# Edge-gated graph layer on one core: edges packed in tiles of 128 per 64 targets instead of a loop over list slots

## The chip, the cores and the metric

The kernel runs on one core of a Trainium2 chip. The metric is the device time of one execution in microseconds (us), as the median of several runs. The profile is one further execution with the hardware profiler on. The core's engines, each with its own instruction stream, are TensorE (PE; its weight loads are listed apart as PEld), VectorE (DVE), ScalarE (ACT), GpSimd (POOL) and SyncE (SP), which here only starts DMAs. SBUF is the on-chip memory, PSUM the memory that TensorE writes its products to, DRAM the memory off the core.

## What is computed

The input `x` holds 16 batches of 1024 nodes with 256 features (h below), in float32; `adj` is a 1024 x 1024 matrix that is zero except for some 9,000 edges.

```python
pre_u = einsum('bud,dk->buk', h, W1[:256])
pre_v = einsum('bvd,dk->bvk', h, W1[256:])
hidden = relu(pre_u[:, :, None, :] + pre_v[:, None, :, :] + b1)
S   = sigmoid(einsum('buvk,ko->buvo', hidden, W2)[..., 0] + b2[0])
a_t = einsum('buv,bud->bvd', S * adj, h)
m_t = einsum('uv,bud->bvd', adj, h) * h
z   = beta1*h + beta2*(a_t @ Wa + ba) + beta3*(m_t @ Wm + bm)
```

The gate S of a pair (u, v) matters only where adj is not zero. With the reference's own inputs there are 9,052 such pairs; the longest list of sources of one target has 19, and of the sixteen groups of 64 consecutive targets the fullest holds 607 edges, the emptiest 549.

## The kernel before

There are two stages. The first runs over the 16 batches. For each it makes three matrix products on TensorE: `pt` (L141: h times W1's upper half and Wa side by side, which goes to `tab` and to a DRAM table of 4 batches), `pp` (L147: h times W1's lower half, which goes to `pv`), and `pm` (L161: the dense product of h with the whole `adj`, 1024 x 1024, which gives m), whose result times Wm (`pz`, L171) makes z except for the gated sum. `pv` and z go to DRAM.

The second stage is the edge loop. It takes 128 targets at a time, one per partition, 8 blocks in all. A hardware loop (L245 to L247) does 4 slots of every target's list in a turn, as many turns as the longest of the 128 lists needs; in the profiled execution that is 35 turns. In a turn VectorE finds the next four sources of each target (`top`, L202; `pick`, L217; `key`, L219). Then come four rounds, one per group of 4 batches. In a round GpSimd starts four indirect DMAs (L211), each of which fetches one row of 8 KB per partition, namely the source's W1 part and its Wa part for 4 batches. VectorE adds `pv` (L223) and, batch by batch, takes relu, multiplies with W2 and sums (L225). ScalarE makes the gate (L228) and, for each batch and slot, a diagonal 128 x 128 matrix `dg` (L235). TensorE multiplies each `dg` with the fetched Wa part and sums into `pa` (L237), 16 products of 128 x 256 a round, and VectorE adds `pa` to z (L238). A partition whose list has ended fetches nothing and weighs 0, but all instructions run over it.

The order of the instructions on each engine is fixed when the program is built, by a scheduler that looks at the dependences and at the buffers of each pool; eight `fetched` buffers and two `pa` buffers are what lets rounds overlap, and nothing overlaps from one turn to the next beyond them. All products are float32, and each is executed as two MATMUL instructions with a weight load each.

Of the kernel before, what the change touches and what calls it, by code (L numbers as in the profile page):

```python
# [13 lines left out]
P = 128  # L14
# [3 lines left out]
def kernel(  # L18
# [32 lines left out]
    HB = 512  # L51
    GB = 4
    NG = B // GB
    TS = 4
    NGB = 8
    assert D == 256 and N % HB == 0
# [4 lines left out]
    table = [dram.tile([N, GB * 2 * D], FP, name=f"table{g}") for g in range(NG)]  # L61
    pv_dram = dram.tile([N, B * D], FP, name="pv_dram")
    z_dram = dram.tile([N, B * D], FP, name="z_dram")

    def rows(src, n):
        return bass.AP(tensor=src.tensor, offset=src.offset, ap=[[0, P], [1, n]])

    def load_rows(src, n, name):
        t = const.tile([P, n], FP, name=name)
        nc.scalar.dma_start(t, rows(src, n))  # L70
        return t
# [3 lines left out]
    adjT_sb = const.tile([P, NT, N], FP, name="adjT_sb")  # L75
    w2_b = load_rows(W2, D, "w2_b")
    b2_b = load_rows(b2, 1, "b2_b")
    turns = const.tile([P, NT], I32, name="turns")
    ukey = const.tile([P, N], FP, name="ukey")
    nc.gpsimd.iota(ukey, pattern=[[-1, N]], base=N, channel_multiplier=0,  # L80
                   allow_small_or_imprecise_dtypes=True)

# [1 line left out]
    with ExitStack() as s1:  # L84
        wp = s1.enter_context(tc.tile_pool(name="wp", bufs=1))
# [44 lines left out]
        for b in range(B):  # L130
            h, hT = hs
            if b + 1 < B:
                hs = load_h(b + 1)
# [107 lines left out]
    for vt in range(NT):  # L241
        pv, z, key = block
        if vt + 1 < NT:
            block = load_block(vt + 1)
# [37 lines left out]
```

## Time and profile before

| | us |
|---|---|
| median of 3 runs | 3558.36 (3556.51 to 3566.06) |
| profiled execution, span | 3569.1 |
| TensorE busy | 2179.8 (61%) |
| VectorE busy | 2148.4 (60%) |
| ScalarE busy | 929.8 (26%) |
| GpSimd busy | 659.6 (18%) |

The profiled execution is 10.7 us (0.3%) longer than the median of the runs. The page cuts the span into 40 slices of 89 us and gives each engine's busy share in tenths. [...] "Idle before" is how long an engine stood still just before the instructions of a group, and the releaser is what ended it. The two stages are easy to tell apart in the slices: TensorE is full in the first eleven, and half full after that.

### The profile page before, as it was taken

What the parts mean: (1) busy time and instruction counts of PE and PEld (TensorE: products, weight loads), DVE (VectorE), ACT (ScalarE), POOL (GpSimd) and SP (SyncE); (2) the same over time, 40 slices, a digit from 0 to 9 for tenths busy, and PEclk for the clock granted to TensorE, in tenths of its full rate; (3) what the DMA queues carried; (4) which work ended last, traced back from release to release, by engine and by line L of the source; (5) the groups of instructions that cost most, each with busy time, mean ns of one, the idle gap of its engine ahead of it and who ended that gap; (6) DMA issues with size and microseconds to landing.
All of it is one profiled execution on the core that took longest, in us unless ns stands there. A gap on an engine that the chain in (4) does not pass through costs nothing. (4 is left out here: it accounts for less than half of the span.)

```text
span 3569.1 us, 27584 instructions
## 1 busy us (share of the span) xinstructions
PE 2179.8 (61%) x7040; PEld 1527.9 (43%) x7040; DVE 2148.4 (60%) x6077; ACT 929.8 (26%) x2672; POOL 659.6 (18%) x568
## 2 busy tenths in 40 slices
PE   8999999999355355445445544555544545535554
PEld 4555555555244244434334433444433434434443
DVE  3122122221776777766877776777678767677776
ACT  1010110110133233333233332333323323323332
POOL 0000000000221322212222222222122322222222
PEclk9999999999667767767677776677666867776777
DMA  6233233322642253063245202530641064135300
GB/s 229 106 133 114 106 106 128 120 106 83 268 188 74 90 208 120 24 257 151 70 182 210 74 15 113 225 131 26 258 162 59 5 237 179 63 123 220 135 15 25
DMA packets 174748, 458.50 MB, mean 128 GB/s; under 512 B 46832, under 2 KB 113904, under 8 KB 136432
## 3 DMA queue, kind: packets, MB, share of 16 engines
q0 software_dynamic: 80640, 296.79, 22.4%
q1 hardware_dynamic: 41888, 92.28, 7.0%
q10 hardware_dynamic: 52160, 68.69, 5.5%
q8 instruction: 30, 0.49, 0.1%
q14 instruction: 30, 0.25, 0.0%
HBM read 664.27 MB, written 83.89 MB: 210 GB/s over the span
## 5 line engine op out<-in xcount | busy, mean ns | idle before, releaser
L237 PE MATMUL pa<-fetched,dg 128*128 128x256 f32 x4480 | 1295.8, 460 | 1363.4 <-ACT dg L235 1363.4
L237 PEld LDWEIGHTS pa<-fetched,dg 128*128 128x128 f32 x4480 | 1046.4, 237 | 1612.8 <-ACT dg L235 1419.7
L211 POOL DMA_INDIRECT fetched<-table,idx x560 | 657.6, 1174 | 2821.8 <-DVE idx L204 1807.5
L225 DVE SCALAR_TENSOR_TENSOR hid<-hid,w_b 128x256 f32<-128x256 f32 x2240 | 823.6, 420 | 15.6
L235 ACT ACTIVATE dg<-ident,wt 128x128 f32<-128x128 f32 x2240 | 744.7, 392 | 282.6 <-PE pa L237 187.8
L223 DVE TENSOR_TENSOR hid<-fetched,pv_blk 128x1024 f32<-128x1024 f32 x560 | 683.0, 1220 | 114.0 <-DMA fetched<-table,idx 111.1
L238 DVE TENSOR_TENSOR z_blk<-pa,z_blk 128x1024 f32<-128x1024 f32 x140 | 171.4, 1224 | 511.2 <-PE pa L237 511.2
L161 PE MATMUL pm<-adj_sb,h 128*128 128x512 f32 x1024 | 442.1, 592 | 0.0
L228 ACT ACTIVATE gate<-sc,b_b 128x16 f32<-128x16 f32 x140 | 43.0, 307 | 1253.6 <-DVE hid L225 1253.5
L161 PEld LDWEIGHTS pm<-adj_sb,h 128*128 128x128 f32 x1024 | 194.6, 190 | 238.1 <-issue 237.3
L163 DVE TENSOR_TENSOR mT<-pm,hT 128x512 f32<-128x512 f32 x64 | 44.2, 691 | 386.7 <-PE pm L161 386.7
L141 PE MATMUL pt<-w_tab,hT 128*128 128x512 f32 x512 | 243.8, 599 | 12.0 <-DMA w_tab<-in_Wa_dram 12.0
L143 ACT ACTIVATE tab<-pt 128x256 f32<-128x256 f32 x128 | 49.2, 384 | 754.4 <-PE pt L141 754.4
L149 DVE TENSOR_TENSOR pv<-pp,b_b 128x256 f32<-128x256 f32 x128 | 54.1, 423 | 240.6 <-PE pp L147 240.6
L217 DVE SCALAR_TENSOR_TENSOR pick<-ukey,top,adjT_sb 128x1024 f32<-128x1024 f32 x140 | 180.1, 1287 | 2.5
L225 DVE DVE_READ_ACCUMULATOR hid<-hid,w_b 128x1 f32 x2240 | 180.2, 80 | 0.0
L147 PE MATMUL pp<-w_v,hT 128*128 128x256 f32 x512 | 131.7, 380 | 3.9 <-DVE pv L149 3.9
L141 PEld LDWEIGHTS pt<-w_tab,hT 128*128 128x128 f32 x512 | 98.2, 192 | 80.9 <-issue 74.3
L228 ACT ACT_TABLE_LOAD x35 | 44.9, 1283 | 321.8 <-DVE hid L225 157.3
L147 PEld LDWEIGHTS pp<-w_v,hT 128*128 128x128 f32 x512 | 97.5, 191 | 72.9 <-issue 61.5
L171 PE MATMUL pz<-w_m,mT 128*128 128x256 f32 x512 | 113.1, 379 | 0.0
L171 PEld LDWEIGHTS pz<-w_m,mT 128*128 128x128 f32 x512 | 91.2, 189 | 26.1 <-issue 7.7
(25 smaller groups left out, 327.0 us busy)
## 6 DMA issues: line engine op xcount, KB each, us to landing
table<-tab ACTq DMA_DIRECT2D x16, 2048.0 KB, 7.0
hT<-in_xT_dram SPq DMA_DIRECT2D x16, 1024.0 KB, 7.4
h<-in_x_dram SPq DMA_DIRECT2D x16, 1024.0 KB, 5.5
pv_dram<-pv ACTq DMA_DIRECT2D x16, 1024.0 KB, 9.4
z_dram<-z ACTq DMA_DIRECT2D x16, 1024.0 KB, 4.4
pv_blk<-pv_dram SPq DMA_DIRECT2D x8, 2048.0 KB, 8.4
z_blk<-z_dram SPq DMA_DIRECT2D x8, 2048.0 KB, 15.0
out_dram<-z_blk SPq DMA_DIRECT2D x8, 2048.0 KB, 37.3
```

Source lines behind the costliest of these rows:

```text
L141: nc.tensor.matmul(pt, hT[:, c, nt * P:(nt + 1) * P], w_tab[:, c, :], start=(c == 0), stop=(c == DC - 1))
L147: nc.tensor.matmul(pp, hT[:, c, nt * P:(nt + 1) * P], w_v[:, c, :], start=(c == 0), stop=(c == DC - 1))
L161: nc.tensor.matmul(pm, h[:, ut, c * P:(c + 1) * P], adj_sb[:, ut, v0:v0 + HB], start=(ut == 0), stop=(ut == NT - 1))
L171: nc.tensor.matmul(pz, mT[:, c, nt * P:(nt + 1) * P], w_m[:, c, :], start=(c == 0), stop=(c == DC - 1))
L211: nc.gpsimd.indirect_dma_start(out=tiles[t], out_offset=None, in_=table[g], in_offset=bass.IndirectOffsetOnAxis(ap=idx[:, t:t + 1], axis=0 ...
L217: nc.vector.scalar_tensor_tensor(pick, ukey, top[:, t:t + 1], adjT_sb[:, vt, :], ALU.is_equal, ALU.mult, accum_out=val[:, t:t + 1])
L223: nc.vector.tensor_tensor(hid, f[:, :, 0, :], pv[:, g * GB:(g + 1) * GB, :], ALU.add)
L225: nc.vector.scalar_tensor_tensor(hid[:, b, :], hid[:, b, :], 0.0, w2_b, ALU.max, ALU.mult, accum_out=sc[:, b, t:t + 1])
L228: nc.scalar.activation(gate, sc, AF.Sigmoid, bias=b2_b)
L235: nc.scalar.activation(dg, ident, AF.Copy, scale=wt[:, b, t:t + 1])
L237: nc.tensor.matmul(pa[:, b, :], dg, f[:, b, 1, :], start=(t == 0), stop=(t == TS - 1))
L238: nc.vector.tensor_tensor(z[:, g * GB:(g + 1) * GB, :], pa, z[:, g * GB:(g + 1) * GB, :], ALU.add)
```

## The change

The dense product with `adj` and the loop over slots are gone. The program is straight-line code for the given shape.

**Lists.** `lists(vt)`, once per block of 128 targets, builds from `adj` the packed lists of its two *windows* of 64 targets. VectorE takes the 24 largest keys of every target (three rounds of `max`); short TensorE products count and place them; each window gets 640 *slots* in 5 tiles of 128, one edge per partition. For every slot there result the source's row number (`uidx`), the edge's value (`val`, fetched from DRAM by ten indirect DMAs of 4 bytes per partition per block), a 0/1 matrix `mark` (which slots belong to which of the 64 targets, kept in DRAM as `who`), and `whose` (slot by target, with the value in it). What does not fit (a list over 24, a window over 640) is done by a loop behind a branch at the end of the program, L372, which is skipped if nothing is left over.

**Tables.** `rows(g, nt)` makes, for 4 batches and 128 nodes, h times W1's halves. The upper half goes to the DRAM table, beside which `copy_h` puts h itself; the lower half stays in SBUF as `pv`, with the targets' two halves swapped for two of the 4 batches (`hs`). Table and `pv` of group g+1 are made during the edges of group g, block by block.

**Edges.** `edges(g, vt, pv)` goes over 2 windows of 5 tiles, 320 tiles in all. Per tile there is one indirect DMA of 128 rows of 8 KB (five `fetched` buffers); two products `pc`, which hand each slot its target's `pv` row, each from 64 partitions only, one from the lower 64 and one from the upper; VectorE's add and four relu-multiply-sums as before; one sigmoid; five ScalarE copies that fill `left` (64 columns with the plain value, 64 with value times gate, for each of 4 batches); and four products into `acc`, which sum m and a side by side (m in 64 of the 128 partitions, a in the other 64). Per window `acc` is read out (`ev`: m times h on VectorE, a on ScalarE) and transposed by 8 TensorE instructions into `LT` (4 ScalarE copies). Per block, 16 products with Wm and Wa give z (L341), which is stored at once.

```diff
-    TS = 4
-    NGB = 8
+    W = 64
+    NW = P // W
+    TW = 5
+    E = TW * P
+    S = 24
...
+    def lists(vt):
...
+        nc.vector.tensor_scalar(key, adj_b, 0.0, None, ALU.not_equal, ALU.add, accum_out=count)
+        nc.vector.tensor_tensor(key, key, ukey, ALU.mult)
+        for s in range(0, S, 8):
+            nc.vector.max(top[:, s:s + 8], key)
+            if s + 8 < S:
+                nc.vector.scalar_tensor_tensor(key, key, top[:, s + 7:s + 8], key, ALU.is_lt, ALU.mult)
...
+        for w in range(NW):
...
+            nc.vector.tensor_scalar(early, slot, Rv[:, 0:1], None, ALU.is_lt)
+            mark = big.tile([P, E], FP, name="mark")
+            nc.vector.scalar_tensor_tensor(mark, slot, first, early, ALU.is_ge, ALU.mult)
+            nc.sync.dma_start(who[i], mark)
...
+            for j in range(TW):
+                nc.gpsimd.indirect_dma_start(
+                    out=val[:, i, j:j + 1], out_offset=None, in_=adj_flat,
...
+            for j in range(TW):
+                nc.vector.tensor_scalar(whose[:, i, j, :], place, L[:, j, 4:5], val[:, i, j:j + 1],
+                                        ALU.is_equal, ALU.mult)
...
+    def rows(g, nt):
...
+        for h in range(2):
+            pu = small("pu")
...
+                    nc.tensor.matmul(pu[:, bb * D:(bb + 1) * D], hT[:, 2 * h + bb, c, :], w_u[:, c, :],
...
+            nc.scalar.copy(tab[:, 2 * h * D:(2 * h + 2) * D], pu)
...
+                    left = hs[:, bb, c, :] if h else hT[:, bb, c, :]
+                    nc.tensor.matmul(pp[:, bb * D:(bb + 1) * D], left, w_v[:, c, :],
...
+        nc.sync.dma_start(table[g][nt * P:(nt + 1) * P, :GD], tab)
...
+    def edges(g, vt, pv):
...
+            for j in range(TW):
...
+                nc.gpsimd.indirect_dma_start(
+                    out=f, out_offset=None, in_=table[g],
...
+                pc = psc.tile([P, 2, 2 * D], FP, name="pc")
+                for h in range(2):
+                    q = (w + h) % 2 * W
+                    nc.tensor.matmul(pc[:, h, :], mark[q:q + W, j * P:(j + 1) * P], pv[q:q + W, h, :],
+                                     start=True, stop=True)
...
+                nc.vector.tensor_tensor(t, f[:, :GD].rearrange("p (b d) -> p b d", b=GB),
+                                        pc.rearrange("p h (b d) -> p (h b) d", b=2), ALU.add)
...
                 for b in range(GB):
...
+                    nc.vector.scalar_tensor_tensor(t[:, b, :], t[:, b, :], 0.0, w2_b,
+                                                   ALU.max, ALU.mult, accum_out=sc[:, b:b + 1])
...
+                nc.scalar.activation(gt, sc, AF.Sigmoid, bias=b2_b)
+                left = wk.tile([P, GB, 2, W], FP, name="left")
+                nc.scalar.activation(left[:, :, w, :], whose[:, i, j, :].unsqueeze(1).to_broadcast([P, GB, W]), AF.Copy)
+                for b in range(GB):
+                    nc.scalar.activation(left[:, b, 1 - w, :], whose[:, i, j, :], AF.Copy, scale=gt[:, b:b + 1])
+                for b in range(GB):
+                    nc.tensor.matmul(acc[:, b, :], left[:, b].rearrange("p k v -> p (k v)"),
...
+            nc.vector.tensor_tensor(ev[m0:m0 + W], acc[m0:m0 + W], hb[m0:m0 + W], ALU.mult)
+            nc.scalar.copy(ev[a0:a0 + W], acc[a0:a0 + W])
...
+                    nc.tensor.transpose(pt[:, k * P:(k + 1) * P], ev[:, b, c * P:(c + 1) * P], ident)
...
+        now, pvs = pvs, []
+        for vt in range(NT):
+            edges(g, vt, now[vt])
+            if g + 1 < NG:
+                pvs.append(rows(g + 1, vt))
```

The pools hold two `pc` buffers, three `left` buffers and one `acc` buffer. In these listings a number behind a name tells buffers of one name apart.

On TensorE, in the edge loop of before, a round's products into one `pa` follow each other, and the next round's come right behind them:

```order
L237 MATMUL pa_5636<-fetched6_2657,dg_5667 128x256
L237 MATMUL pa_5636<-fetched7_2659,dg_5670 128x256
L237 MATMUL pa_5636<-fetched4_2653,dg_5673 128x256
L237 MATMUL pa_5636<-fetched5_2655,dg_5676 128x256
L237 MATMUL pa_5636<-fetched6_2657,dg_5679 128x256
L237 MATMUL pa_5636<-fetched7_2659,dg_5682 128x256
L237 MATMUL pa_5727<-fetched0_2645,dg_5728 128x256
L237 MATMUL pa_5727<-fetched1_2647,dg_5731 128x256
```

Nothing stands between two rounds there; each product hangs on its own `dg`.

On TensorE now, in the middle of a block's edges (`acc_8078` and `acc_8223` are its first and second window, five `left` tiles each; L302 with x2 is one tile's `pc`, without it half a tile's):

```order
L318 MATMUL acc_8078<-fetched3_173,left_8169 128x256 x4
L302 MATMUL pc_8253<-pv_5610,mark_8221 128x512 x2
L302 MATMUL pc_8278<-pv_5610,mark_8221 128x512
L318 MATMUL acc_8078<-fetched4_175,left_8194 128x256 x4
L302 MATMUL pc_8278<-pv_5610,mark_8221 128x512
L302 MATMUL pc_8303<-pv_5610,mark_8221 128x512 x2
L329 MATMUL misc_8207<-ident_108,ev_8204 128x128 x4
L329 MATMUL misc_8214<-ident_108,ev_8204 128x128 x4
L318 MATMUL acc_8223<-fetched0_167,left_8239 128x256 x4
L318 MATMUL acc_8223<-fetched1_169,left_8264 128x256 x4
L318 MATMUL acc_8223<-fetched2_171,left_8289 128x256 x4
L318 MATMUL acc_8223<-fetched3_173,left_8314 128x256 x4
```

The products of a tile now stand apart from the `pc` they depend on: up to three tiles' `pc` stand ahead of the sums that need them, and the transposes (L329) stand behind more `pc`.

On VectorE, in the edge loop of before (the start of a turn's first two rounds):

```order
L223 TENSOR_TENSOR hid_5517<-fetched0_2645,pv_blk_5073 128x1024
L225 SCALAR_TENSOR_TENSOR hid_5517,sc_5499<-hid_5517,w2_b_72 128x256 x4
L223 TENSOR_TENSOR hid_5523<-fetched1_2647,pv_blk_5073 128x1024
L225 SCALAR_TENSOR_TENSOR hid_5523,sc_5499<-hid_5523,w2_b_72 128x256 x4
L223 TENSOR_TENSOR hid_5529<-fetched2_2649,pv_blk_5073 128x1024
L225 SCALAR_TENSOR_TENSOR hid_5529,sc_5499<-hid_5529,w2_b_72 128x256 x4
L223 TENSOR_TENSOR hid_5535<-fetched3_2651,pv_blk_5073 128x1024
L225 SCALAR_TENSOR_TENSOR hid_5535,sc_5499<-hid_5535,w2_b_72 128x256 x4
L223 TENSOR_TENSOR hid_5608<-fetched4_2653,pv_blk_5073 128x1024
L230 TENSOR_TENSOR wt_5543<-gate_5541,val_5497 128x16
L225 SCALAR_TENSOR_TENSOR hid_5608,sc_5595<-hid_5608,w2_b_72 128x256 x4
```

Add and sums alternated slot by slot, and a round's 16 sums all came before its gate.

On VectorE now, at the same place of the block as the TensorE listing (`t_8186` is the first window's last tile, `t_8231` to `t_8306` are the second window's first four):

```order
L305 TENSOR_TENSOR t_8186<-fetched4_175,pc_8183 128x1024
L305 TENSOR_TENSOR t_8231<-fetched0_167,pc_8228 128x1024
L309 SCALAR_TENSOR_TENSOR t_8186,sc_8188<-t_8186,w2_b_86 128x256 x4
L309 SCALAR_TENSOR_TENSOR t_8231,sc_8233<-t_8231,w2_b_86 128x256 x4
L305 TENSOR_TENSOR t_8256<-fetched1_169,pc_8253 128x1024
L309 SCALAR_TENSOR_TENSOR t_8256,sc_8258<-t_8256,w2_b_86 128x256 x3
L323 TENSOR_TENSOR ev_8204<-acc_8078,h_blk_8073 64x1024
L309 SCALAR_TENSOR_TENSOR t_8256,sc_8258<-t_8256,w2_b_86 128x256
L305 TENSOR_TENSOR t_8281<-fetched2_171,pc_8278 128x1024
L305 TENSOR_TENSOR t_8306<-fetched3_173,pc_8303 128x1024
L309 SCALAR_TENSOR_TENSOR t_8281,sc_8283<-t_8281,w2_b_86 128x256 x4
L309 SCALAR_TENSOR_TENSOR t_8306,sc_8308<-t_8306,w2_b_86 128x256 x4
```

VectorE now takes two tiles' adds before their sums, and the read-out of the first window (`ev`, L323) stands behind the add and three sums of the second window's second tile.

## Rows read from the trace of the kernel before

**Rows 1.** The page's head, its first part (busy time by engine) and second (40 slices).

```profile
span 3569.1 us, 27584 instructions
...
PE 2179.8 (61%) x7040; PEld 1527.9 (43%) x7040; DVE 2148.4 (60%) x6077; ACT 929.8 (26%) x2672; POOL 659.6 (18%) x568
...
PE   8999999999355355445445544555544545535554
...
PEclk9999999999667767767677776677666867776777
```

**Rows 2.** Busy time by stretch: matrix products, then edge loop.

```profile
core 0: us, PE busy (x) PEld busy (x) DVE busy (x) ACT busy (x) POOL busy (x), PEclk, DMA share, GB/s
...
500.00:900.00 400.00, 399.90 (x1171) 219.07 (x1169) 88.03 (x156) 41.94 (x112) 0.00 (x0) 1.00 0.30 105
...
1500.00:2500.00 1000.00, 493.49 (x1705) 398.64 (x1706) 730.72 (x2170) 317.63 (x924) 245.89 (x210) 0.72 0.35 130
```

**Rows 3.** The edge loop in order of time: start, length, engine, line.

```profile
1499.77 1.22 DVE L223 TENSOR_TENSOR hid<-fetched,pv_blk 128x1024 f32<-128x1024 f32 x1
...
1502.42 0.08 DVE L225 DVE_READ_ACCUMULATOR hid<-hid,w_b 128x1 f32 x1
...
1502.53 0.31 ACT L228 ACTIVATE gate<-sc,b_b 128x16 f32<-128x16 f32 x1 [8.33 <-DVE hid L225]
...
1503.82 3.03 ACT L235 ACTIVATE dg<-ident,wt 128x128 f32<-128x128 f32 x10 [0.98 <-DVE wt L230]
...
1504.27 10.07 PE L237 MATMUL pa<-fetched,dg 128*128 128x256 f32 x32 [7.05 <-ACT dg L235]
```

**Rows 4.** TensorE alone in order of time: four rounds of the loop.

```profile
2011.02 9.30 PE L237 MATMUL pa<-fetched,dg 128*128 128x256 f32 x32 [22.30 <-ACT dg L235]
2023.71 7.17 PE L237 MATMUL pa<-fetched,dg 128*128 128x256 f32 x32 [3.40 <-ACT dg L235]
...
2050.83 9.87 PE L237 MATMUL pa<-fetched,dg 128*128 128x256 f32 x32 [3.39 <-ACT dg L235]
2083.00 9.15 PE L237 MATMUL pa<-fetched,dg 128*128 128x256 f32 x32 [22.30 <-ACT dg L235]
```

**Rows 5.** Groups of instructions by line: busy, mean ns, idle before, releaser.

```profile
L237 PE MATMUL pa<-fetched,dg 128*128 128x256 f32 x4480 | 1295.8, 460 | 1363.4 <-ACT dg L235 1363.4
...
L211 POOL DMA_INDIRECT fetched<-table,idx x560 | 657.6, 1174 | 2821.8 <-DVE idx L204 1807.5 <-PE pa L237 752.7 <-issue 114.9
L161 PE MATMUL pm<-adj_sb,h 128*128 128x512 f32 x1024 | 442.1, 592 | 0.0
...
L238 DVE TENSOR_TENSOR z_blk<-pa,z_blk 128x1024 f32<-128x1024 f32 x140 | 171.4, 1224 | 511.2 <-PE pa L237 511.2
...
L171 PE MATMUL pz<-w_m,mT 128*128 128x256 f32 x512 | 113.1, 379 | 0.0
...
L163 DVE TENSOR_TENSOR mT<-pm,hT 128x512 f32<-128x512 f32 x64 | 44.2, 691 | 386.7 <-PE pm L161 386.7
...
L143 ACT ACTIVATE tab<-pt 128x256 f32<-128x256 f32 x128 | 49.2, 384 | 754.4 <-PE pt L141 754.4
...
L202 DVE MAX8 top<-key 128x8 f32<-128x1024 f32 x35 | 42.9, 1225 | 29.7 <-PEq L247 28.5 <-PEq L245 1.2
...
L230 DVE TENSOR_TENSOR wt<-gate,val 128x16 f32<-128x16 f32 x140 | 23.9, 171 | 28.6 <-ACT gate L228 28.6
```

**Rows 6.** The instructions on tile pz: duration min, median, max.

```profile
L171 PEld LDWEIGHTS pz<-w_m,mT x512: 186/190/190, 67.2 to 899.3; 128*128 128x128 f32 x171
L171 PE MATMUL pz<-w_m,mT x512: 379/379/379, 67.6 to 899.5; 128*128 128x256 f32 x171
```

**Rows 7.** The DMA queues and issues: KB each, us to landing.

```profile
q0 software_dynamic: 80640, 296.79, 22.4%
...
table<-tab ACTq DMA_DIRECT2D x16, 2048.0 KB, 7.0
...
fetched<-table,idx POOLq DMA_INDIRECT x560, 5.7
```

More of the change, by code (lines that the diff above doesn't have):

```diff
@@ L62 @@
[L62 to L66, printed above, removed]
+    table = [dram.tile([N, 2 * GD], FP, name=f"table{g}") for g in range(NG)]
+    who = [dram.tile([P, E], FP, name=f"who{w}") for w in range(NT * NW)]
+    adj_flat = adjT.rearrange("v (u one) -> (v u) one", one=1)
+    x_rows = x.rearrange("b n d -> n b d")
+    xT_rows = xT.rearrange("b (c p) n -> p (b c) n", p=P)
@@ L199, in turn @@
-    def turn(vt, pv, z, key):
-        top = wk.tile([P, 8], FP, name="top")
-        nc.vector.max(top, key)
-        idx = wk.tile([P, TS], I32, name="idx")
-        nc.vector.tensor_scalar(idx, top[:, :TS], -1.0, float(N), ALU.mult, ALU.add)
-        val = wk.tile([P, TS], FP, name="val")
-        pick = wk.tile([P, N], FP, name="pick", bufs=1)
-        for g in range(NG):
-            tiles = [fetched[(g * TS + t) % NGB] for t in range(TS)]
-            sc = wk.tile([P, GB, TS], FP, name="sc")
-            for t in range(TS):
+    turn = [0]
@@ new lines, in edges @@
+    def edges(g, vt, pv):
+        hb = big.tile([P, GB, D], FP, name="h_blk")
+        nc.sync.dma_start(hb, x_rows[vt * P:(vt + 1) * P, g * GB:(g + 1) * GB, :])
+        LT = wk.tile([P, GB * DC, 2, P], FP, name="LT", bufs=1)
+        for w in range(NW):
+            i = vt * NW + w
+            mark = big.tile([P, E], FP, name="mark")
+            nc.sync.dma_start(mark, who[i])
+            acc = psa.tile([P, GB, D], FP, name="acc")
+            for j in range(TW):
+                n = turn[0]
+                turn[0] += 1
+                f = fetched[n % NF]
+                gt = wk.tile([P, GB], FP, name="gt")
@@ L238, in turn @@
-            nc.vector.tensor_tensor(z[:, g * GB:(g + 1) * GB, :], pa, z[:, g * GB:(g + 1) * GB, :], ALU.add)
-    block = load_block(0)
[L241 to L244, printed above, removed]
-        n_turns = nc.values_load(turns[0:1, vt:vt + 1], min_val=1, max_val=N // TS,
-                                 skip_runtime_bounds_check_because="a count of at most N, in turns of TS, at least 1")
-        with tc.For_i(0, n_turns, 1):
-            turn(vt, pv, z, key)
-        nc.sync.dma_start(out[:, vt * P:(vt + 1) * P, :].rearrange("b p d -> p b d"), z)
+                pc = psc.tile([P, 2, 2 * D], FP, name="pc")
@@ new lines, in edges @@
+        nc.sync.dma_start(out[g * GB:(g + 1) * GB, vt * P:(vt + 1) * P, :].rearrange("b p d -> p b d"), z)
+    copy_h(0)
+    pvs = []
+    for nt in range(NT):
+        pvs.append(rows(0, nt))
+        lists(nt)
+    for g in range(NG):
+        if g + 1 < NG:
+            copy_h(g + 1)
+        now, pvs = pvs, []
+        for vt in range(NT):
+            edges(g, vt, now[vt])
+            if g + 1 < NG:
+                pvs.append(rows(g + 1, vt))
+    main.close()
+    longest = const.tile([P, NT], FP, name="longest")
@@ new lines @@
+    nc.gpsimd.partition_all_reduce(longest, rest, P, bass_isa.ReduceOp.max)
+    most = const.tile([P, 1], FP, name="most")
+    nc.vector.tensor_reduce(most, longest, AX.X, ALU.max)
+    turns = const.tile([P, NT + 1], I32, name="turns")
+    nc.vector.tensor_copy(turns[:, :NT], longest)
+    nc.vector.tensor_copy(turns[:, NT:], most)
+    any_left = nc.values_load(turns[0:1, NT:NT + 1], min_val=0, max_val=N,
+                              skip_runtime_bounds_check_because="a count of at most N")
```

370 lines of the change are left out of this document (243 added, 127 removed).

## The prediction

> **What bounds the kernel now.** I read the page's slices first, then the stretches, the loop in order of time, and last the prices by line. The span falls into two stages. Up to 900 us TensorE makes the matrix products: it is busy in 399.9 of 400 us at a granted clock of 1.00 [rows 2], and the last `pz` product starts at 899.5 [rows 6]. Then comes the edge loop, where neither VectorE (73% busy) nor TensorE (49%, mean clock 0.72) is full [rows 1, 2]. In order of time the reader sees why: VectorE works through four slots, ScalarE makes the gate and then the diagonals, TensorE does its 32 instructions in 7.2 to 9.9 us, VectorE waits for them (511.2 us in all) and adds `pa` to z [rows 3 to 5]. TensorE stands still 1363.4 us for `dg` [rows 5]. A turn takes 72.0 us (2083.00 - 2011.02) [rows 4], and 35 turns (`top` x35) [rows 5] make 2520 of the 3569.1 us; some 150 go into block changes. The loop handles 35 x 4 x 128 = 17,920 slots for 9,052 edges: half of its work is for ended lists.
>
> **What goes.** The dense product `pm` (442.1 us busy [rows 5]) goes altogether, being replaced by columns that stand beside the gated sum. The loop's 560 slot rounds become 320 tiles, 10,240 slots for the same edges. Rows fetched are the same edges' rows, so the fetch queue's 296.8 MB stay [rows 7]. The branch at the end isn't taken with these inputs (longest list 19 of 24, fullest window 607 of 640).
>
> **One tile, engine by engine.** TensorE: `pc` is two products of 512 columns, four instructions at 442.1/1024 = 0.432 us, 1.73 us; the sums are four products of 256 columns, eight instructions at 7.17/32 = 0.224 us, 1.79 us [rows 4, 5]. Together 3.52 us. VectorE: add and four sums took 2.65 us from one start to the next (1499.77 to 1502.42) and do the same work now, from PSUM, which cost the same in L238 (1224 ns) [rows 3, 5]. ScalarE: gate 0.31, five copies at about 0.3 (ten diagonals took 3.03 us), the widest nearer 0.47: 2.0 us [rows 3]. GpSimd: one fetch, 1.17 us [rows 5]. So TensorE is the slowest, and the others are covered by it: over a block of 128 targets VectorE has 10 x 2.65 and some 6.5 us of read-outs, 33 us, ScalarE about 27, GpSimd about 14.
>
> **One block on TensorE.** Ten tiles 35.2. Two times 8 transposes: no row shows one, so between one and two weight loads of 0.19 each [rows 6], plus 0.16 for the end of each half (a product ends 379 - 221 = 158 ns after the next has begun [rows 5, 6]): 1.8 to 3.3 a window. I take 1.8, as a transposing instruction is one, not two; 3.6. The 16 products with Wm and Wa: 32 x 0.221 = 7.1 [rows 5]. The next group's 16 in `rows`: 7.1. Sum 53.0; in the last group, without `rows`, 45.9.
>
> **Does TensorE wait?** A tile's sums need, from the end of its `pc`: 0.16, VectorE 2.73 (1499.77 to 1502.50), the gate 0.03 + 0.31, the first copy and hand-over 0.45 (1503.82 to 1504.27): 3.68 us [rows 3]. The change's order decides what lies between. I lay the listed rows end to end, from the start of the first window's fourth sums (0). TensorE then does the second window's `pc` 1 and half of 2 until 4.4. VectorE has taken the adds of the fifth tile and of the next window's first by 1.6 and the fifth's sums by 3.0, so its `left` is there at 3.8: no wait. Sums until 6.2, then `pc` 2 and 3 until 8.7. `ev` starts at 6.7, behind the second tile's add and three sums, and ends at 7.9, before the transposes need it. They end at 10.5, and the next four tiles' sums follow at 1.8 us each, with their `left` ready 0.2 to 2 us ahead; three `pc` follow, and the fifth tile's sums wait some 0.15. The three `left` buffers hold a copy back until the sums three tiles earlier are through, which in this order is never the last thing. So TensorE is nearly full. With margins of a few tenths in several places I add 1 us a block for slips: 54.0, and 46.9 without `rows`. 24 x 54.0 + 8 x 46.9 = 1671 us.
>
> The fetches stay hidden: five buffers give a fetch four tiles' time, some 21 us, for 1.17 + 5.7 us [rows 5, 7]. The fetch queue took 22.4% of 3569.1 us of all 16 engines, 800 us [rows 7], about half of the new time; the rest of the traffic is some 115 MB. If a fetch took over 21 us, each tile would wait for it.
>
> **Around the edges.** (a) *Lists.* By the nearest rows VectorE spends, per block, five 1024-wide passes at 1.22 (L238) and three `max` at 1.23 (10 us), four 640-wide (0.8 each by width, 3), two adds of 512 columns at 0.69 (1.4), and some 45 small instructions at 0.17 (7.7): 21 to 22 us [rows 5]. The ten value fetches cost GpSimd 11.7 us, and the last lands up to 5.7 later [rows 5, 7]; `whose` waits for them, with about 8 us of other VectorE work in between: 9 more. 30 x 8 = 240 us; the bounds are 170 (fetches wholly covered) and 307 (nothing between). TensorE has little to do in it, and nothing covers this part: the first edges need the whole table of their group. For the first loads I add 12, two landings as in [rows 7]. (b) *Three changes of group.* The next table's last rows are made behind the last block's z, then copied (about 0.6), stored (7.0 at most), fetched (1.17 + 5.7), and go the 3.68 us way; TensorE has some 4 us of work meanwhile and afterwards begins at the lower clock, as after the loop's long gaps (9.15 against 7.17) [rows 4, 5, 7]: 17 each, 51. (c) The end: the last z's add (0.69) and store (7.0 at most) [rows 5, 7], and the branch, in all 15.
>
> Sum: 1671 + 240 + 12 + 51 + 15 = 1989, against the profiled execution's 3569.1. The median of the runs lies 0.3% under that, so 1983, say **1985 us**.
>
> **Clock.** [...] In the loop, after a gap of 3.40 us 32 instructions took 7.17 us once and, after 3.39, 9.87 another time [rows 4]: gaps of this length are where the level sometimes falls. My gaps inside the edges are well under that, so I price them at the upper level.
>
> **Rivals.** *(A) The two `pc` products run side by side.* One uses the lower 64 partitions, the other the upper, and they write different halves of `pc`. No row shows such a pair. In the order the halves stand in runs of 5, 3, 3, 6 and 3 per block; if neighbours overlapped, a run of n would take n + 1 instruction times instead of 2n, 25 instead of 40, 15 x 0.432 = 6.5 us less; the 3.68 us way would take about 2 back. 32 x 4.5 = 145: 1840 us. For it: nothing in the dependences forbids it; against it: in all rows TensorE's products succeed each other. [...]
>
> *(B) Changing between 64- and 128-partition products costs a stop.* At each end of those five runs TensorE would finish (0.16) and load weights uncovered (0.19) [rows 5, 6]: 10 x 0.35 x 32 = 112, so 2097 us; two-load transposes would add up to 96. [...] In rows, where all products have 128 partitions, a product starts before the one ahead has ended, so they neither confirm it nor refute it.
>
> *(C) The order doesn't hold, and every tile goes its way alone.* If TensorE stood still the whole 3.68 us before each tile's sums but for one `pc`, a tile would take 3.68 + 1.79 = 5.5 us, 320 x 2.0 = 640 more: 2620 us. For it speaks the loop of before, where VectorE and TensorE do wait for each other; against it that `pc` now stands two to three tiles ahead.
>
> *(D) Slower than before: the clock stays at its lower level all through the edges.* The products' 24 x 53.0 + 8 x 45.9 = 1639 us would double to 3278, with the other terms 3596, by the median's 0.3% some 3585 us. It decides at a mean granted clock of 0.50 over the edges (1639/0.50 + 318 = 3596); the loop of before had 0.72 with TensorE half idle [rows 2], so I give it little.
>
> **How the numbers follow.** Forecast (1900 to 2080) 0.42; A, 1780 to 1900, 0.25; B, 2080 to 2230, 0.18; C and other waits, 2230 to 3500, 0.09; below 1780 0.02; D 0.04. The range takes in A with the long lists' bound and B with the two-load transposes: 1810 to 2230. About 0.3% is what a measurement of this kernel can tell from no change. Faster 0.95, within 0.3% 0.01 (only D brushes it), slower 0.04.
>
> **What would show it.** TensorE's share of a stretch of edges should be above 0.9 with the clock near 1.00, and the groups `acc` and `pc` should have about 0.22 and 0.43 us busy per instruction; under 0.3 for `pc` is A. The first `acc` should start near 250 us, a block should take 54 us, and the three changes of group should be gaps of 15 to 20 us on TensorE. Much idle time of TensorE released by ScalarE's `left` would be C, a clock below 0.8 in the edges D's beginning. The forecast is wrong if GpSimd's fetches or the lists take more than their bounds, since nothing covers those.

## The result and the profile after

The changed kernel takes 1948.0 us (median; 1946.4 to 1954.2) against 3562.2 us of the kernel before in the same session: a ratio of 0.547 with a 95% interval of 0.546 to 0.548. Its profiled execution has a span of 1944.6 us. The head of its page, to be read against [rows 1] (the row PEclk is TensorE's granted clock in tenths of full speed):

```profile
span 1944.6 us, 22106 instructions
...
PE 1590.1 (82%) x6640; PEld 1116.4 (57%) x6640; DVE 1193.9 (61%) x3595; ACT 726.4 (37%) x2306; POOL 442.1 (23%) x479
...
PE   1456459998888879999888879999998878989996
...
PEclk9676579999999989999999989999999989999999
```

The slices show three things. The dense stage is gone. The first six slices (some 290 us) are the lists, with TensorE half idle. After them TensorE is the fullest engine, with three notches, the changes of group, at each of which the clock's digit falls too. In place of 511.2 us in which VectorE waited for TensorE and 1363.4 in which TensorE waited for ScalarE [rows 5], these are now the groups by line (busy us, mean ns of one, idle before it and its releasers):

```profile
L318 PE MATMUL acc<-fetched,left 128*128 128x256 f32 x2560 | 623.1, 394 | 78.8 <-ACT left L316 78.0
L302 PE MATMUL pc<-pv,mark 64*128 64x512 f32 x1280 | 404.2, 636 | 66.3 <-DVE t L305 59.7 <-DMA mark<-who 6.6
L305 DVE TENSOR_TENSOR t<-fetched,pc 128x1024 f32<-128x1024 f32 x320 | 383.5, 1216 | 318.0 <-PE pc L302 285.9 <-DMA fetched<-table,uidx 30.4 <-issue 0.5
L329 PE MATMUL misc<-ident,ev 128*128 128x128 f32 x512 | 71.4, 283 | 52.1 <-ACT ev L324 52.1
```

Two prices differ from the forecast at once: `pc` is 404.2/1280 = 0.316 us busy per instruction (forecast 0.43), and TensorE's idle time is spread over ScalarE's `left` (78), VectorE's `t` (60) and the read-out `ev` (52). TensorE alone in order of time, around one end of a window:

```profile
1030.62 1.13 PE L302 MATMUL pc<-pv,mark 64*128 64x512 f32 x4 [0.46 <-DVE t L305]
1032.91 1.99 PE L318 MATMUL acc<-fetched,left 128*128 128x256 f32 x8 [1.16 <-ACT left L316]
1034.83 1.98 PE L302 MATMUL pc<-pv,mark 64*128 64x512 f32 x6
1036.74 1.99 PE L318 MATMUL acc<-fetched,left 128*128 128x256 f32 x8
1038.67 1.98 PE L302 MATMUL pc<-pv,mark 64*128 64x512 f32 x6
1042.14 1.09 PE L329 MATMUL misc<-ident,ev 128*128 128x128 f32 x8 [1.49 <-ACT ev L324]
```

The four instructions of a whole tile's `pc` take 1.13 us where four one behind the other would take 1.73 + 0.16 by the prediction's prices. Of six, two belong to a tile whose other half stands behind the next sums, and they take 1.98. The 1.49 us ahead of the transposes end a read-out in two steps, VectorE's half and then ScalarE's:

```profile
1039.83 1.21 DVE L323 TENSOR_TENSOR ev<-acc,h_blk 64x1024 f32<-64x1024 f32 x1
...
1041.08 1.01 ACT L324 COPY ev<-acc 64x1024 f32<-64x1024 f32 x1 [1.79 <-DVE ev L323]
```

A block of 128 targets takes 51.3 us (its z is stored at 966.02, 1017.36 and 1068.69). The change of group:

```profile
696.79 0.69 DVE L262 TENSOR_TENSOR pv<-misc,b_b 128x512 f32<-128x512 f32 x1 [1.57 <-PE misc L260]
...
701.59 1.02 POOL L295 DMA_INDIRECT fetched<-table,uidx  x1 [1.23 <-DMA table<-tab]
...
707.59 1.22 DVE L305 TENSOR_TENSOR t<-fetched,pc 128x1024 f32<-128x1024 f32 x1 [10.11 <-DMA fetched<-table,uidx]
708.87 2.07 PE L302 MATMUL pc<-pv,mark 64*128 64x512 f32 x2 [12.11 <-DVE t L305]
...
711.23 3.78 PE L318 MATMUL acc<-fetched,left 128*128 128x256 f32 x8 [0.29 <-ACT left L316]
```

Store, fetch and VectorE follow one another with nothing beside them, TensorE stands 12.1 us, and its next sums take 3.78 us instead of 1.99, at a granted clock of 0.53 (711.2 to 715.1 us).

### The profile page after: what moved, and what is told of

Read it like the earlier page. It is cut to its first block, busy times and chain, and to the rows that moved or that the text cites. A ratio compares the mean times of both kernels' runs of the same rounds, so it can differ in the third digit from the quotient of the medians.

```text
span 1944.6 us, 22106 instructions
## 1 busy us (share of the span) xinstructions
PE 1590.1 (82%) x6640; PEld 1116.4 (57%) x6640; DVE 1193.9 (61%) x3595; ACT 726.4 (37%) x2306; POOL 442.1 (23%) x479
## 5 line engine op out<-in xcount | busy, mean ns | idle before, releaser
L318 PE MATMUL acc<-fetched,left 128*128 128x256 f32 x2560 | 623.1, 394 | 78.8 <-ACT left L316 78.0
L318 PEld LDWEIGHTS acc<-fetched,left 128*128 128x128 f32 x2560 | 483.0, 195 | 248.5 <-ACT left L316 179.0
L295 POOL DMA_INDIRECT fetched<-table,uidx x320 | 326.3, 1020 | 1195.4 <-PE acc L318 982.4
L305 DVE TENSOR_TENSOR t<-fetched,pc 128x1024 f32<-128x1024 f32 x320 | 383.5, 1216 | 318.0 <-PE pc L302 285.9
L309 DVE SCALAR_TENSOR_TENSOR t<-t,w_b 128x256 f32<-128x256 f32 x1280 | 471.2, 423 | 18.4 <-DVE t L305 0.5
L302 PE MATMUL pc<-pv,mark 64*128 64x512 f32 x1280 | 404.2, 636 | 66.3 <-DVE t L305 59.7
L316 ACT ACTIVATE left<-whose,gt 128x64 f32<-128x64 f32 x1280 | 347.6, 339 | 9.5
L302 PEld LDWEIGHTS pc<-pv,mark 64*128 64x128 f32 x1280 | 130.3, 189 | 246.9 <-issue 119.7
L253 PE MATMUL misc<-w_u,hT 128*128 128x256 f32 x512 | 135.7, 413 | 24.4 <-DMA hT<-in_xT_dram 24.4
L341 PE MATMUL misc<-w_m,LT 128*128 128x256 f32 x512 | 138.5, 394 | 1.7 <-ACT LT L332 0.3
L341 PE MATMUL misc<-w_a,LT 128*128 128x256 f32 x512 | 132.7, 382 | 0.0
L329 PEld LDWEIGHTS misc<-ident,ev 128*128 128x128 f32 x512 | 55.8, 142 | 103.3 <-ACT ev L324 103.3
L329 PE MATMUL misc<-ident,ev 128*128 128x128 f32 x512 | 71.4, 283 | 52.1 <-ACT ev L324 52.1
L341 PEld LDWEIGHTS misc<-w_m,LT 128*128 128x128 f32 x512 | 96.6, 194 | 25.2 <-ACT LT L332 13.1
```

Source lines behind the costliest of these rows:

```text
L253: nc.tensor.matmul(pu[:, bb * D:(bb + 1) * D], hT[:, 2 * h + bb, c, :], w_u[:, c, :], start=(c == 0), stop=(c == DC - 1))
L295: nc.gpsimd.indirect_dma_start(out=f, out_offset=None, in_=table[g], in_offset=bass.IndirectOffsetOnAxis(ap=uidx[:, i, j:j + 1], axis=0), ...
L302: nc.tensor.matmul(pc[:, h, :], mark[q:q + W, j * P:(j + 1) * P], pv[q:q + W, h, :], start=True, stop=True)
L305: nc.vector.tensor_tensor(t, f[:, :GD].rearrange("p (b d) -> p b d", b=GB), pc.rearrange("p h (b d) -> p (h b) d", b=2), ALU.add)
L309: nc.vector.scalar_tensor_tensor(t[:, b, :], t[:, b, :], 0.0, w2_b, ALU.max, ALU.mult, accum_out=sc[:, b:b + 1])
L316: nc.scalar.activation(left[:, b, 1 - w, :], whose[:, i, j, :], AF.Copy, scale=gt[:, b:b + 1])
```

## The experiments

Differences below are of ratios to the kernel before, times 3562 us. "The order of TensorE" is the sequence of its instructions in the built program; in the changed kernel it passes 374 times between 64-row and 128-row products, and 67 of the 320 tiles are torn, that is, have other products between their two `pc`.

**Do the two `pc` products run side by side, and what does a change of form cost?** Two kernels with the same order of TensorE as the changed one, word for word (only the rows that `pc`, and in the second also one short product of the lists, read differ). First, both products on the same 64 rows:

```diff
-                                  hT[:, 2:4, :, (1 - w) * W:(2 - w) * W])
+                                  hT[:, 2:4, :, w * W:(w + 1) * W])
...
-                    q = (w + h) % 2 * W
+                    q = w * W
```

> Both 64-row products of a tile read the same 64 partitions (the half of `hs` isn't swapped, and both read the rows of their own window); everything else is that of the changed kernel, and so is the result. In the changed kernel a tile's four pc instructions take 1.13 us together. Theory (the two products of a tile run side by side because they lie on different rows): here they follow one another, four take 1.7 to 1.9 us, TensorE's busy time rises by 320 x 0.6 to 0.75 = 190 to 240 us, of which its waiting (some 190 us in the loop) takes up a part, and the time rises by 80 to 220 us, to 2030 to 2170. Rival (64-row products are simply that short, whatever rows they are on): no change, 1935 to 1960, and four still take 1.13 us.

Measured: 2021.5 us, ratio 0.566 (0.564 to 0.568), 67 us more than the changed kernel, less than the 80 that the theory asked for. Second, all 128 rows, half of them zeros:

```diff
+            nc.vector.tensor_scalar(early, slot, Rv[:, 0:1], half[:, w:w + 1], ALU.is_lt, ALU.mult)
...
+                    nc.tensor.matmul(pc[:, h, :], mark[:, j * P:(j + 1) * P], pv[:, h, :],
```

> The mark of a window is zero in the other window's 64 rows, and each pc product reads all 128 rows, so that TensorE never changes between 64-row and 128-row products in the loop; nothing runs side by side. Compared with the run that keeps both products on the same 64 rows. Theory (a change between the two forms costs little): the same time as that run within 15 us, four instructions 1.7 to 1.9 us. [...]

Measured: 1957.9 us, ratio 0.548 (0.547 to 0.550): the same as the changed kernel within the interval, and 63 us less than with the same rows, where the theory asked for the same time within 15. TensorE in order of time, with the same rows and then with all rows:

```profile
1015.53 1.99 PE L318 MATMUL acc<-fetched,left 128*128 128x256 f32 x8 [0.31 <-ACT left L316]
1017.45 2.84 PE L302 MATMUL pc<-pv,mark 64*128 64x512 f32 x6
1020.22 1.99 PE L318 MATMUL acc<-fetched,left 128*128 128x256 f32 x8
...
1032.85 1.99 PE L302 MATMUL pc<-pv,mark 64*128 64x512 f32 x8
1036.14 2.08 PE L302 MATMUL pc<-pv,mark 64*128 64x512 f32 x4 [1.30 <-DVE t L305]
1038.43 3.40 PE L318 MATMUL acc<-fetched,left 128*128 128x256 f32 x8 [0.21 <-ACT left L316]
```

```profile
1005.55 5.31 PE L304 MATMUL pc<-pv,mark 128*128 128x512 f32 x12
1011.03 1.99 PE L320 MATMUL acc<-fetched,left 128*128 128x256 f32 x8 [0.17 <-ACT left L318]
...
1042.10 2.74 PE L304 MATMUL pc<-pv,mark 128*128 128x512 f32 x6
1044.67 1.89 PE L320 MATMUL acc<-fetched,left 128*128 128x256 f32 x8
1046.40 2.74 PE L304 MATMUL pc<-pv,mark 128*128 128x512 f32 x6
```

The first theory holds in part, the second does not. Products on different rows do run side by side: six `pc` take 2.84 us on the same rows and 1.98 on alternating ones. The first listing shows it a second time: eight `pc` in a row take 1.99 us, because there the last tile of one block (upper rows) stands next to the first of the next (lower rows). And a change of form has a price: one run of six `pc` and one of eight sums take 4.69 us from start to start (1015.53 to 1020.22) where without a change they take 4.30 (1042.10 to 1046.40): 0.39 for two, 0.2 us a change.

The 63 us between the two kernels are not that price alone. Where eight `pc` ran side by side, TensorE comes to the next `pc` before VectorE has freed its buffer and waits 1.30 us; the next sums take 3.40 us there, as the changed kernel's do at a granted clock of 0.50 (3.33 us at 1308.33), and 1.99 at the same place with all rows (1011.03). Over 700 to 1100 us the mean granted clock is 0.96 with the same rows and 0.98 with all rows. Since the order is the same, the two traces can be laid side by side, instruction by instruction: some 41 of the 68 us by which they differ from the first `pc` on lie in stretches where only the run with the same rows has the lower clock.

In the same way the changed kernel, laid beside the run with all rows, gains some 87 us inside its runs of `pc`, loses 62 at the changes of form (their price and the waits that stand there, together) and 23 in stretches where only it has the lower clock. That is why pairing and plain 128-row products come out alike.

The pairing's 169 us of TensorE's busy time (1759.4 to 1590.1) came back as 77 of span: these are TensorE's groups of the run with the same rows, where the waits for `left` and `ev` were 21 and 9 us in place of 79 and 52.

```profile
L318 PE MATMUL acc<-fetched,left 128*128 128x256 f32 x2560 | 638.2, 401 | 21.2 <-ACT left L316 20.8
L302 PE MATMUL pc<-pv,mark 64*128 64x512 f32 x1280 | 567.2, 619 | 75.2 <-DVE t L305 68.6 <-DMA mark<-who 6.6
L329 PE MATMUL misc<-ident,ev 128*128 128x128 f32 x512 | 70.8, 282 | 9.4 <-ACT ev L324 9.4
```

So more than half of the gain became a wait for the chain VectorE to ScalarE, which the slower `pc` had covered.

**Is the read-out in two steps on the path?**

```diff
-            nc.vector.tensor_tensor(ev[m0:m0 + W], acc[m0:m0 + W], hb[m0:m0 + W], ALU.mult)
-            nc.scalar.copy(ev[a0:a0 + W], acc[a0:a0 + W])
+            nc.vector.tensor_tensor(ev, acc, hbx[w], ALU.mult)
```

> One VectorE instruction reads the whole sums (times h in the m half, times one in the a half: two tiles of which one half is preset to one and the other loaded by DMA), instead of VectorE's half and behind it ScalarE's. Theory (the read-out one after the other, 1.22 + 1.01 us at each of 64 window ends, is on TensorE's path): a window's sums are free 1.0 us earlier, TensorE's idle time at the transposes (52.1 us) falls below 25, and the time falls by 35 to 65 us, to 1885 to 1915. Rival (the wait only moves, to ScalarE's `left` or to the pc buffers): within 15 us of the changed kernel.

Measured: 1963.2 us, ratio 0.550 (0.548 to 0.552), 10 us more. TensorE's wait for `ev` stayed at 49.8 us. It settles nothing: the scheduler laid TensorE's order anew, with 119 torn tiles and 412 changes, and put the transposes earlier. At 0.43 to 0.86 us for each of 52 more torn tiles and 0.2 for each of 38 more changes, that costs an estimated 30 to 52 us, about what the ScalarE copy could bring. So the rival, too, is neither shown nor refuted.

**Is the change of group the wait for the table?**

```diff
-            edges(g, vt, now[vt])
             if g + 1 < NG:
                 pvs.append(rows(g + 1, vt))
+            edges(g, vt, now[vt])
```

> The block `rows` of the next group stands ahead of each target block instead of behind it, so that the last piece of the next group's table is stored one block (some 50 us) before the first fetch from it. Theory (the 12.1 us in which TensorE waits at the change of groups, and the low clock behind it, are the wait for store and first fetch): the three changes lose 12 to 17 us each, the time falls by 30 to 50 us, to 1900 to 1920. Rival (the first fetches wait for the buffers of the last tiles anyway, or the wait is for something other than the table): within 10 us.

Measured: 1894.7 us, ratio 0.532 (0.530 to 0.533), 56 us less, 19 for each change of group; VectorE's wait for fetches fell from 30.4 to 3.4 us and the clock's slices show no notch. The theory holds, though the gain is above its 30 to 50 us. From one block's last sums to the next one's the first two changes of group take 68.7 and 68.4 us in the changed kernel and 51.3 here. The order also has only 326 changes of form here, but the blocks within a group take as long as before, so the gain isn't there.

**Keeping pairs together.** Higher priority for `pc`, and then two tiles' `pc` in one piece:

```diff
+                with tc.high_priority():
                     for h in range(2):
...
```

> The run with `rows` ahead (1894.7), and the two pc products of a tile have a higher priority than all else: in the order of TensorE only 2 of 320 tiles then have other products between their two (66 there), but TensorE changes between 64-row and 128-row products 634 times (326 there). Theory (a change costs 0.17 us: the 64 us between the runs with the same rows and with all rows, over 374 changes; a pair that is torn apart costs the 0.43 to 0.86 us that its halves save side by side): +52 from the changes, -28 to -55 from the pairs, so 1890 to 1920. Rival (changes cost nothing and the waits for pc and `left` are what is left): the pairs come earlier, so 1830 to 1865.

```diff
-    psc = main.enter_context(tc.tile_pool(name="psc", bufs=2, space=bass.MemoryType.PSUM))
+    psc = main.enter_context(tc.tile_pool(name="psc", bufs=1, space=bass.MemoryType.PSUM))
...
+                if n % 2 == 0:
+                    two = psc.tile([P, 2, 2, 2 * D], FP, name="pc")
+                    with tc.high_priority():
+                        for e in range(2):
...
```

> The run with `rows` ahead (1894.7), and the pc products of two tiles issue together into one set of four banks: no tile is torn, and TensorE changes its form 320 times (326 and 66 torn there). Theory (as above): -28 to -55 from the pairs, nothing from the changes, so 1840 to 1867, if VectorE is not left without pc. Rival (with one set of four banks pc waits until VectorE has read both tiles, and VectorE then waits for pc): 160 waits of 0.5 us or more, the gain is gone, 1890 to 1980.

Measured: 2147.7 us (ratio 0.603) and 2115.2 us (0.594), far above what either theory allowed. What VectorE does in the first one, at the end of a block, and TensorE at the same time:

```profile
1014.54 0.69 DVE L262 TENSOR_TENSOR pv<-misc,b_b 128x512 f32<-128x512 f32 x1 [1.57 <-PE misc L260]
1024.62 1.22 DVE L306 TENSOR_TENSOR t<-fetched,pc 128x1024 f32<-128x1024 f32 x1 [9.38 <-DMA fetched<-table,uidx]
```

```profile
1012.62 1.89 PE L260 MATMUL misc<-w_v,hs 128*128 128x256 f32 x8
1014.35 8.80 PE L319 MATMUL acc<-fetched,left 128*128 128x256 f32 x40
1025.89 1.13 PE L303 MATMUL pc<-pv,mark 64*128 64x512 f32 x4 [2.75 <-DVE t L306]
```

VectorE waits for a fetch, 406.6 us in all (3.4 in the run that this one changes). With `pc` always first, VectorE finishes five tiles while TensorE does 14 us of z products and `rows`; the sums of all five tiles (x40) stand behind those, all five `fetched` buffers are held until then, and the sixth fetch starts too late. The clock goes with the waits: its mean over the span is 0.877, against 0.938 in the run that this one changes. In the second run VectorE waits 274.5 us for fetches and, as its rival had it, 214.2 for `pc`. GpSimd's `hs` copies, which stood ahead of those fetches in its queue and waited 586 us for hT, were a second suspect:

```diff
-            nc.gpsimd.tensor_copy(hs[:, :, :, w * W:(w + 1) * W],
-                                  hT[:, 2:4, :, (1 - w) * W:(2 - w) * W])
+            nc.sync.dma_start(hs[:, :, :, w * W:(w + 1) * W].rearrange("p b c n -> p (b c) n"),
+                              xT_rows[:, (g * GB + 2) * DC:(g + 1) * GB * DC, at:at + W])
```

> The run with the higher priority for pc (2147.7), and `hs` is loaded by two DMAs per block straight from xT in place of two GpSimd copies. Theory (in that run the `hs` copies stand ahead of the fetches in GpSimd's queue and wait there for the load of hT, 586 us over 25 blocks; the fetches behind them start late and VectorE waits for them, 407 us): the first fetch of a block starts some 4 us earlier, the time falls by 60 to 150 us, to 2000 to 2090. Rival (the five buffers are held by products that stand behind the 14 us of z products and `rows`, whatever the queue's order): VectorE's wait for fetches stays above 350 us, the time within 40 us of 2147.7.

Measured: 2108.1 us (ratio 0.591), 41 us less, between the two expectations, and VectorE's wait for fetches is 407.8 us, as before. The queue's order was a small part; the held buffers are left as a suspect. If they are the cause, the 14 us in a row must go:

```diff
+    for n in range(NTILE):
...
+        if n + 2 < NTILE:
+            pc_of(n + 2)
+            score(n + 2)
+        if rgen and s in (0, 1, 2, 3):
+            next(rgen)
...
+        if b > 0 and s in (1, 2, 3, 5):
+            next(zgen)
+        if s == 5:
+            turn_sums(b * NW)
+        sums(n)
+        if n + NF < NTILE:
+            fetch(n + NF)
```

> The order of TensorE written by hand: per tile the two pc products of two tiles ahead, a piece of other work, and the tile's sums; the z products of the last block and the `rows` of the next group go in pieces of eight instructions, one or two per tile, in place of 14 us in a row; six fetch buffers; `hs` by DMA. No tile is torn, TensorE changes its form 636 times. Theory (what held the runs with kept pairs was the 14 us in a row, behind which five tiles' buffers stay held): a block of 128 targets takes 10 x (1.05 + 1.73 + 0.34) + 13.8 + 2.2 = 47.2 us and two waits of 0.5 us for the read-out, where the run with `rows` ahead takes 51.4; so 1894.7 less 28 x 3.2 to 4.2, 1775 to 1805, and at the changes of groups up to 8 us each on top, at most 1830. Rival (the 636 changes and the in-order waits cost what the kept pairs bring): 1870 to 1920.

Measured: **1777.2 us, ratio 0.499 (0.498 to 0.501)**, half of the time before and the fastest of all. TensorE in order of time:

```profile
1022.28 1.13 PE L342 MATMUL pc<-pv,mark 64*128 64x512 f32 x4
1023.34 1.99 PE L371 MATMUL acc<-fetched,left 128*128 128x256 f32 x8
1025.26 1.13 PE L342 MATMUL pc<-pv,mark 64*128 64x512 f32 x4
1026.32 1.99 PE L371 MATMUL acc<-fetched,left 128*128 128x256 f32 x8
```

There is no gap, the clock is 1.00 from 300 to 1700 us, and TensorE is busy in 1328 of these 1400 us; VectorE waits 2.5 us for fetches. A block takes 48.1 us (47.2 and two waits of 0.5 expected). This run has six buffers, short pieces, `hs` by DMA and whole pairs all at once (and, smaller, `left`'s plain copy ahead of the sigmoid and a higher priority for the read-out), so it agrees with the picture without saying what each is worth; that the held buffers alone were the cause is not shown. A tile takes 2.98 us (1023.34 to 1026.32) for products worth 2.59 (0.86, two of the 0.43 that each of six takes with all rows, 1042.10 to 1044.67; 1.73, eight of `rows` from start to start with pairs kept, 1012.62 to 1014.35): 0.39 for two changes, again 0.2 us each.

**Half the changes, by hand.**

```diff
+        if s in (2, 8):
+            two_tiles(n + 2)
...
+            turn_sums(b * NW, lambda: two_tiles(n + 1))
```

> The run with the hand-written order (1777.2), with the pc products of two tiles issued one behind the other, so that TensorE changes its form 320 times in place of 636, and two pieces of other work ahead of the transposes of a window, whose two halves stand on either side of a pc pair. Theory (a tile there takes 2.98 us from pc to pc, where its products are worth 2.59, so a change costs 0.2 us; the transposes waited 72 us in all): 316 x 0.2 = 62 us from the changes and up to 50 from the waits, 1665 to 1725. Rival (VectorE, 2.65 us a tile, becomes the bound or leaves pc late, since both pc buffers fall free together): 1740 to 1800.

Measured: 1915.0 us, ratio 0.537 (0.536 to 0.538), 133 us more than the run before it: what the missing changes are worth in time was not tested, since another wait came in, and with it the mean granted clock fell from 0.948 to 0.889. Of the waits by engine and releaser (us, times, longest):

```profile
DVE z L405 <- DMA out_dram<-z: 143.5, 30, 5.9
...
PE pc L342 <- DVE t L352: 137.3, 31, 6.2
```

VectorE's first instruction on a new `z` needs the buffer of the z before last, and stands in its queue right behind that z's last add; so all later tiles wait until the store has landed, 7.9 us in the median here. In the run before it stands in the same place, but there the store lands in 2.9 us, and the wait is 0.6 us in all. The store here meets those of `tab` and the loads of hT on SP's queue; that this is what slows it was not tried, nor was a third `z` buffer.

**The start.**

```diff
-    nc.vector.memset(val, 0.0)
+    nc.vector.memset(val, 0.12)
...
-            for j in range(TW):
-                nc.gpsimd.indirect_dma_start(
-                    out=val[:, i, j:j + 1], out_offset=None, in_=adj_flat,
...
```

> The changed kernel without the 80 fetches of the edge weights (every weight is 0.12, so the output differs; the `whose` rows are still made). Theory (in the start stage a list's chain goes through the ten fetches of 1.0 us with 0.3 us between, 13 us of the 29.4 us of a list): the first product of edges comes at 185 to 215 us in place of 275.7, the time falls by 60 to 90 us, to 1858 to 1888. Rival (VectorE's own chain for the next list takes the 29.4 us, the fetches lie beside it): first product at 265 to 276, within 12 us.

```diff
+        nc.sync.dma_start(tab[:, GD:].rearrange("p (b d) -> p b d", b=GB),
+                          x_rows[nt * P:(nt + 1) * P, g * GB:(g + 1) * GB, :])
...
-        nc.sync.dma_start(table[g][nt * P:(nt + 1) * P, :GD], tab)
+        nc.sync.dma_start(table[g][nt * P:(nt + 1) * P, :], tab)
```

> `rows` loads h into the second half of `tab` and stores whole table rows, in place of the four 4 MB copies of h from DRAM to DRAM, three of which run in the first 60 us beside the first loads (DMA share 0.96 there, the first hT waited for 24.4 us). Theory (these copies hold up the start): the first product of edges comes 20 to 35 us earlier than 275.7 us, the time falls by 15 to 35 us, to 1913 to 1933. Rival (the lists' own chain sets the start and takes up any gain): within 8 us.

The third changes the run with half the changes by hand (1915.0), which is "the run beside it":

```diff
         lists(nt)
+        weigh(earlier)
```

> The same, and in the start stage the `whose` rows of a list are made one list later, so that VectorE doesn't wait there for the edge weights (46 us in the run before). Theory (this wait is part of the 29.4 us of a list): the first product of edges 15 to 40 us earlier than in the run beside it, and the time 15 to 40 us lower. Rival (the ten fetches and the chain of the list set the period, as without the fetches it still took 25 us): within 8 us.

Measured, first `pc` and time: without the fetches 238.2 us and 1915.1 us (36 less); with h in `tab` 260.0 us and 1943.8 us (8 less, at the edge of what the intervals tell apart); `whose` one list later 242.4 us against 269.4 in the run beside it, and 1886.5 us against 1915.0. So the value fetches cost 37 us, between the two expectations, and most of it (27 us in the third run, as its theory had it) is VectorE standing in its queue for a value that the next list doesn't need. The early copies of h cost 16 us at the start, but storing whole rows loses much of it again later: the two profiled spans are alike (1945.2 and 1944.6). Part of the loss is at the changes of group, where TensorE then stands up to 15.0 us instead of 12.1; the rest was not traced.

## Why the prediction was right

1985 us was forecast and 1948 measured; the range held it, and the direction was never in doubt. Part by part, though, the sum holds by terms that cancel, so much of the closeness is luck. Of the forecast's 1989 us for the profiled execution, 252 were the start, 1722 the edges with the changes of group, and 15 the end. The trace has 276 to the first `pc`, 1660 from there to the last product of z (275.7 to 1935.5), and 9 after it.

- **`pc`, 1.73 us a tile: wrong, A took place.** A whole pair takes 1.13 us. The rival's mechanism was right; its price, 6.5 us a block off the products and 2 back, was too large. Against the run with the same rows, which still pairs at the ends of blocks, TensorE's busy time falls by 169 us, but the waits for `left` and `ev` grow by 101, and 77 us of span are left. The sign that the forecast gave for A, under 0.3 us busy per instruction, was just missed (0.316), with 67 tiles torn. Six `pc` take 1.98 us on alternating rows and 2.84 on the same ones.
- **Changes of form at no cost: wrong as well, B took place too.** The forecast's rival priced 320 changes at 0.35, 112 us; measured in place, 0.2 us each, 374 are an estimated 75. That TensorE finishes its products there (0.16) and loads weights uncovered (0.19) was the rival's estimate; the runs show the price, not what it is made of. A and B, weighed as alternatives, came together and, with the waits and the lower clock behind them, left nothing: plain 128-row products do as well as these pairs.
- **Waits of 1 us a block: too small.** From 300 to 1850 us TensorE waited 68 us for `left`, 48 for `ev` and, group changes apart, some 22 for `t` (58 less 36): 138 us over some 30 blocks, 4.6 a block. The forecast had `ev` done before the transposes needed it; ScalarE's half starts only when VectorE's has ended, so the read-out takes 2.2 us, not 1.2.
- **Transposes, 1.8 us a window: too dear.** 1.09 measured, 45 us less in all, and below the forecast's lower bound, which was 1.8.
- **Block: 54.0 forecast, 51.3 measured**; these four meet in it.
- **Lists, 30 us each: right (29.4, from the first `max` at 40.8 us to the first `pc`)**, with the right reason, a wait for the value fetches not wholly covered, but partly by luck: without the fetches a list still takes 25 us where 21 to 22 were forecast, and the fetches add 37 us over eight lists, 4.6 each, where 9 were forecast. **First loads, 12 us: wrong**, the first sums come at 282, not near 250; the copies of h for three later groups were issued in the first 60 us (DMA share 0.96 there) and the first hT came at 24 us. Without these copies the first `pc` comes 16 us earlier.
- **Changes of group, 17 us: right**; taking them away gave 17 to 19 each.
- **Clock:** near 1.00 in the edges (0.95 to 0.99 by stretch), as forecast; D, all edges at 0.50, the level that the loop of before has from 1500 to 1504 us, did not come. But the reason was wrong: the forecast took gaps well under 3.4 us to leave the level alone. In the changed kernel it fell behind waits of 0.46 and 1.16 us (granted clock 0.50 from 1309 to 1312 us, the sums 3.33 us instead of 1.99), while the same two waits at 1030 us left it alone (1.00 from 1030.6 to 1034.9 us, the sums 1.99 us):

```profile
1306.05 1.13 PE L302 MATMUL pc<-pv,mark 64*128 64x512 f32 x4 [0.46 <-DVE t L305]
1308.33 3.33 PE L318 MATMUL acc<-fetched,left 128*128 128x256 f32 x8 [1.16 <-ACT left L316]
```

- **The range:** its ends do not follow from the sums that it names. A with the long lists' bound is 1840 + 67 = 1907, B with the two-load transposes 2097 + 96 = 2193; 1810 and 2230 have no working. TensorE's share of a stretch of edges, forecast above 0.9, was 0.88 to 0.90.

## What to carry to other kernels

When two mechanisms with opposite signs rest on the same feature (here row halves: side by side, but with a change of form), give them a joint case and not two chances that exclude each other. Before a gain on the fullest engine is booked, ask which chain it was covering: 169 us of TensorE's time were worth 77 of span. Before a difference between two runs is divided by a count to make a price, look where in the trace the difference lies: 41 of the 68 us above lay in stretches of lower clock. A priority that lets one engine run ahead turned here into late fetches behind a long block of other work; the order by hand, with short pieces between the tiles among its changes, gave 115 us where the priorities lost time.

## What the runs showed of the hardware

- Two fp32 products of 64 rows by 512 columns on different row halves ran side by side (changed kernel, four instructions in 1.13 us), also when they belong to different tiles (run with the same rows, eight in 1.99); on the same half they followed one another (same run, six in 2.84).
- A change between 64-row and 128-row products cost some 0.2 us, in two separate readings (4.69 us with the same rows against 4.30 with all rows, for two; 2.98 us in the order by hand against products worth 2.59, for two).
- A transposing fp32 instruction of 128 columns came every 0.12 us (changed kernel, eight in 1.09, the last one's end included), about half of a 256-column product instruction's 0.22 (forty in 8.80).
- TensorE's granted clock fell to 0.50 behind waits of 0.46 and 1.16 us (changed kernel, 1309 to 1312 us; eight sums took 3.33 us instead of 1.99), but not each time (the same two waits at 1030 us: clock 1.00, 1.99 us). Behind a wait of 1.30 us (run with the same rows) eight sums took 3.40 us.
